# Feed-forward matmuls by one level of Strassen, in a transformer block of linear attention and a Hadamard feed-forward

## The chip, the cores and the metric

The kernel runs on one core of one Trainium2 chip, in float32. The metric is the device time of one execution in microseconds (us), the median over several runs. A profile is one more execution, with a record of every instruction; its span is close to the runs' time. Engines are named as the profile names them: PE is TensorE (matmuls), PEld its weight loads, DVE is VectorE, ACT is ScalarE, POOL is GpSimd, SP is SyncE, which here issues every DMA.

## What is computed

A sequence of 4096 tokens of width 512 goes through linear attention (16 heads of 128, 4 key/value heads), a residual and a layer norm, then a feed-forward with Hadamard transforms, a residual and a second layer norm. The attention is not touched by the change. The feed-forward of the reference, cut to what matters:

```python
def fwht(x):                      # normalised Walsh-Hadamard transform over the last dim
    ...
x = fwht(x * SU_ug) / SCALE       # 4096 x 512
x_up = x @ W_up.T * (Wscale_ug[:INTER] * SCALE)      # INTER = 2048
x_gate = x @ W_gate.T * (Wscale_ug[INTER:] * SCALE)
x = jax.nn.silu(x_gate) * x_up
x = fwht(x * SU_dp) / SCALE       # 4096 x 2048
x = x @ W_down.T * (Wscale_dp * SCALE)               # 4096 x 512
...
x = _layernorm(x + ffn(x))
```

## The kernel before

Float32 precision is had from three passes[...]: each operand is split into a high part (ScalarE copies and rounds it) and a low part (VectorE or GpSimd subtracts), and high x high, high x low and low x high are summed in PSUM. `hilo` (L89) is that split; it appears as L90 (ScalarE) and L91 (the subtraction) in the profile.

There are three stages. Attention runs first (projections at L239 for q and k with 128x256 moving operands, L192 for v, scores and state at L289 to L367); it leaves its numerators, denominators and reciprocals in DRAM (`num_d`, `den_d`, `rec_d`). Then the output projection loops over 32 tiles of 128 tokens (L610): 48 matmuls each at L622 out of resident weights, residual, first norm, and the result to `y_d` in DRAM. Beside it, GpSimd and VectorE prepare the down weights: `prep_down` (L576) transforms `W_down` along its 2048 inputs (a 128x128 Hadamard matmul at L589 and L590, then four butterfly steps on GpSimd at L598), so that the second transform is not done on activations, and puts the split weights into `wdn_d`.

The feed-forward loops over 8 blocks `f` of 512 tokens (L658), and inside over 16 tiles `it` of 128 hidden units (L661). `front` (L495) prepares a block's input: it reads `y_d`, does the 512-wide Hadamard transform by nine butterfly steps of adds and subtractions on VectorE or GpSimd (L509, L510), transposes on TensorE (L518) and splits. For each `it`, `load_wug` (L522) reads the gate/up weights and splits them, anew in every block; 24 matmuls at L682 give gate and up, ScalarE does the silu (L687), VectorE the product (L688), and the result is split and kept. At the end of a block, 192 matmuls at L707 multiply it with the resident down weights `WD`, 48 in each of four chains over the whole 2048; residual, second norm and output follow at L713 to L715. Activations of the hidden layer never leave the chip's on-chip memory.

The order on each engine is not the program's: a scheduler places the instructions by a timeline of its own, and each engine then runs its list in order, waiting on semaphores. The DMAs of all stages go through one queue, issued by SP in its own fixed order. Buffers are pools of a fixed number of tiles (`wres` has 28 tiles of 256 KB, `praw` 3), and an instruction that writes a tile waits for the last reader of the tile that was there before.

Of the kernel before, what the change touches and what calls it, by code (L numbers as in the profile page):

```python
# [21 lines left out]
TF = 512  # L22
NF = NTOK // TF
EPS_DEN = 1e-6
EPS_LN = 1e-5
# [3 lines left out]
LAG = 1  # L29


def rsqrt_small(nc, pool, v, tag):
    y = pool.tile([128, 1], F32, tag=tag + "y", name=tag + "y")
    a = pool.tile([128, 1], F32, tag=tag + "a", name=tag + "a")
    nc.vector.tensor_scalar(y.bitcast(I32), v.bitcast(I32), 1, None, ALU.logical_shift_right)
    nc.vector.tensor_scalar(y.bitcast(I32), y.bitcast(I32), -1.0, float(0x5F3759DF), ALU.mult, ALU.add)
    c, f = 3.0, 1.0
    for _ in range(3):
        nc.vector.tensor_scalar(a, y, y, v, ALU.mult, ALU.mult)
        nc.vector.scalar_tensor_tensor(y, a, c, y, ALU.subtract, ALU.mult)  # L40
        f = f * -0.5 if c == 3.0 else f / (-2.0 * c / 3.0)
        c = 3.0 / (f * f)
    nc.vector.tensor_scalar(y, y, f, None, ALU.mult)
    return y
# [3 lines left out]
def kernel(  # L48
# [28 lines left out]
    wdn_d = dram.tile([16, 128, 2, 512], F32, name="wdn_d")  # L77
# [413 lines left out]
    suug = mid.tile([128, DM], F32, name="suug")  # L491
    wsc = mid.tile([128, 2, 16], F32, name="wsc")
    Y, YT = {}, {}

    def front(pool, fpool, nb, ptr, f, t, eng):  # L495
        if t == 0:
            Y[f] = []
        y = pool.tile([128, DM], F32, tag="y", name="y")
        dma(y, y_d[4 * f + t])
        Y[f].append(y)  # L500
        yield
        a = fpool.tile([128, DM], F32, tag="fw0v" if eng is V else "fw0g", name="fw0", bufs=1)
        b = fpool.tile([128, DM], F32, tag="fw1", name="fw1", bufs=nb)
        eng.tensor_tensor(a, y, suug, ALU.mult)  # L504
        w = 1
        while w < DM:
            aa = a.rearrange("p (n r w) -> p n r w", r=2, w=w)
            bb = b.rearrange("p (n r w) -> p n r w", r=2, w=w)
            eng.tensor_tensor(bb[:, :, 0], aa[:, :, 0], aa[:, :, 1], ALU.add)  # L509
            eng.tensor_tensor(bb[:, :, 1], aa[:, :, 0], aa[:, :, 1], ALU.subtract)  # L510
            a, b = b, a
            w *= 2
        yield
        if t == 0:
            YT[f] = tuple(mid.tile([128, 4, TF], F32R, tag="yT", name=n, bufs=2) for n in ("yTh", "yTl"))
        ps = ptr.tile([128, 4, 128], F32, tag="tr", name="ps_tr")
        for k in range(4):
            T.transpose(ps[:, k], a[:, k * 128:(k + 1) * 128], idt)  # L518
        h, l = (z[:, :, t * 128:(t + 1) * 128] for z in YT[f])
        hilo(h, l, ps)  # L520

    def load_wug(it):  # L522
        w = mid.tile([128, 2, 2, 4, 128], F32R, tag="wug", name="wug_s", bufs=2)
        wf = w.rearrange("p l u k m -> p l (u k m)")
        for j in range(2):
            c = slice(j * 512, (j + 1) * 512)
            hilo(wf[:, 0, c], wf[:, 1, c], load_raw(wug[it, :, c]))
        return w

    def layer_norm(pool, x, o, tag):  # L530
        bs = pool.tile([128, 6], F32, tag="bs", name="bs")
        mv = pool.tile([128, 2], F32, tag="mv", name="mv")
        vv = pool.tile([128, 1], F32, tag="vv", name="vv")
        V.bn_stats(bs, x)
        V.bn_aggr(mv, bs)
        V.tensor_scalar(vv, mv[:, 1:2], EPS_LN, None, ALU.add)
        rs = rsqrt_small(nc, pool, vv, tag)
        V.tensor_scalar(o, x, mv[:, 0:1], rs, ALU.subtract, ALU.mult)

# [1 line left out]
    with ExitStack() as es:  # L541
        p2 = es.enter_context(tc.tile_pool(name="c2", bufs=2, reuse_waits="tile"))
        p1 = es.enter_context(tc.tile_pool(name="c1", bufs=1, reuse_waits="tile"))
# [5 lines left out]
        def norm_o(t, g):  # L549
# [3 lines left out]
            hi, lo = (p2.tile([128, 4, 128], F32R, tag="o", name=n, bufs=10) for n in ("oh", "ol"))  # L553
# [4 lines left out]
        for h in (NH - 2, NH - 1):  # L558
            WO.append(load_w(wo[h], mid, bufs=4))
        for g in range(KVH):  # L560
            norm_o(0, g)
        dma(suug, su_ug.partition_broadcast(128))
        dma(wsc, ws_ug)
        V.tensor_scalar(wsc, wsc, float(1.0 / np.sqrt(np.float32(DM))), None, ALU.mult)
        had32 = p1.tile([128, 128], F32, name="had32")
        dma(had32, had)
        hadr = p1.tile([128, 128], F32R, name="hadr")
        V.tensor_copy(hadr, had32)
        sudp = p1.tile([128, 16], F32, name="sudp")
        dma(sudp, su_dp)  # L570
        V.tensor_tensor(wsc[:, 0], wsc[:, 0], sudp, ALU.mult)
        wsdp = p1.tile([128, DM], F32, name="wsdp")
# [3 lines left out]
        def prep_down(q):  # L576
            raw = p2.tile([128, 16, 64], F32, tag="da", name="draw")
            dma(raw, wd[q])
            yield
            h = p1.tile([128, 2, 16, 64], F32R, tag="dh", name="dh")  # L580
            for j in range(2):
                c = slice(8 * j, 8 * j + 8)
                hilo(h[:, 0, c], h[:, 1, c], raw[:, c])
            yield
            a = p2.tile([128, 16, 64], F32, tag="db", name="dbf")
            for j in range(2):
                c = slice(8 * j, 8 * j + 8)
                ps = pfd.tile([128, 8, 64], F32, tag="fd", name="ps_fd")
                T.matmul(ps, hadr, h[:, 0, c], start=True, stop=False)  # L589
                T.matmul(ps, hadr, h[:, 1, c], start=False, stop=True)  # L590
                V.tensor_tensor(a[:, c], ps, wsdp[:, None, q * 64:(q + 1) * 64].to_broadcast([128, 8, 64]), ALU.mult)
            for step in range(1, 5):
                w = 1 << (step - 1)
                b = p2.tile([128, 16, 64], F32, tag="da" if step % 2 else "db", name="dbf")
                aa = a.rearrange("p (n r w) d -> p n r w d", r=2, w=w)
                bb = b.rearrange("p (n r w) d -> p n r w d", r=2, w=w)
                for r, op in ((0, ALU.add), (1, ALU.subtract)):
                    G.tensor_tensor(bb[:, :, r], aa[:, :, 0], aa[:, :, 1], op)  # L598
                a = b
            yield  # L600
            hl = p1.tile([128, 2, 16, 64], F32R, tag="dh", name="dhl")
            for j in range(2):
                c = slice(8 * j, 8 * j + 8)
                hilo(hl[:, 0, c], hl[:, 1, c], a[:, c])
            for j in range(2):
                dma(wdn_d[:, :, j, q * 64:(q + 1) * 64].rearrange("i p d -> p i d"), hl[:, j])

        fins, gd, ug = [], [], []
        starts = (0, 4, 8, 12, 16, 20, 23, 26)
        for t in range(32):  # L610
            if t + 2 < 32:
                pre(t + 2)
            else:
                ug.append(load_wug(t - 30))
# [13 lines left out]
            yt = p2.tile([128, DM], F32, tag="yt", name="yt")  # L628
            layer_norm(p2, xn, yt, "r1")
            dma(y_d[t], yt)  # L630
            if t in starts:
                gd.append(prep_down(len(gd)))
            for q, t0 in enumerate(starts):
                if t - t0 in (0, 1, 2):
# [138 lines left out]
```

## Time and profile before

| what | us |
|---|---|
| median of 3 runs | 2407.45 (2407.33 to 2408.84) |
| span of the profiled execution | 2408.2 |
| attention, to the first output projection matmul | 941 |
| output projection, to the first gate/up matmul | 376 |
| feed-forward, first of eight blocks | 150 |
| one of the later blocks | 133.65 |
| from the last matmul to the end | 7.7 |

The blocks are read from the chain of work that ended last, in which each block's first gate/up matmul can be found (1316.84, 1467.30, 1600.73, 1734.38). A "span" is from the first to the last instruction. Busy time of matmuls is modelled, since they are pipelined: a matmul of 128x512 is shown with 392 ns although the next one starts 227 ns after it. So the distance of the starts is what counts. A group of instructions is shown as line, engine, operation, output<-inputs, count, busy time, mean, and then the idle time just before it:

```
L91 DVE TENSOR_TENSOR wug_s<-raw,wug_s 128x512 fp32r<-128x512 f32 x256 | 181.3, 743 | 11.4 <-ACT wug_s L90 11.3
L688 DVE SCALAR_TENSOR_TENSOR hh<-ps_gu,wsc,sg 128x512 f32<-128x512 f32 x128 | 95.9, 749 | 269.1 <-PE ps_gu L682 267.9 <-ACT sg L687 1.2
L300 DVE TENSOR_TENSOR s<-ps_s,s 128x256 f32<-128x256 f32 x124 | 51.9, 419 | 14.7 <-PE ps_s L289 13.5
L713 DVE TENSOR_TENSOR y<-ps_dn,y 128x512 f32<-128x512 f32 x32 | 22.0, 689 | 94.4 <-PE ps_dn L707 94.1
L598 POOL TENSOR_TENSOR dbf<-dbf 128x512 f32<-128x512 f32 x64 | 97.5, 1544 | 196.7 <-DVE dbf L591 184.2 <-issue 7.2 <-DVE mv L535 4.2
L221 POOL TENSOR_TENSOR sw<-sw,csb 128x512 f32<-128x512 f32 x160 | 217.2, 1358 | 166.8 <-ACT sw L220 158.5 <-POOL A L346 1.5 <-DVE A L343 0.8
```

### The profile page before, as it was taken

To read this page: it belongs to the slowest core of one execution; us is meant where nothing else is said; L and a number is where in the kernel's file an instruction comes from. 1 tells how busy PE (TensorE), PEld (TensorE's weight loads), DVE (VectorE), ACT (ScalarE), POOL (GpSimd) and SP (SyncE) were. 2 spreads that over 40 slices of the span, in tenths; PEclk is the share of its full clock that TensorE was granted. 3 is DMA by queue.
4 is the path that set the end of the run, shared out by engine and by line. 5 is a ranking of instruction groups with operands and counts; after the bars stand their busy time and mean duration, and the time that the engine had idled before them with its cause. 6 is when DMAs were issued, how large, how long until landed. Compare 5 with 4: busy or idle time off the path is not lost.

```text
span 2408.2 us, 38221 instructions
## 1 busy us (share of the span) xinstructions
PE 2356.0 (98%) x13600; PEld 2040.2 (85%) x13600; DVE 1825.2 (76%) x3408; ACT 1106.5 (46%) x1928; POOL 848.6 (35%) x839
## 2 busy tenths in 40 slices
PE   7999999999999998999999899999999999999998
PEld 6999999999999996777888688888888888888887
DVE  6999999998888897999998847475655757475443
ACT  5777777777777774222222332314141323324140
POOL 2455454454444452684242504022220405031000
PEclk9999999999999998999999899999999999999999
DMA  6555555644554447878885532213131222223120
GB/s 181 144 157 147 176 145 151 170 132 133 140 146 137 125 135 244 285 235 274 272 275 176 177 131 76 92 60 98 44 114 59 91 70 88 83 70 95 42 92 18
DMA packets 223583, 329.97 MB, mean 137 GB/s; under 512 B 62398, under 2 KB 99328, under 8 KB 219424
## 3 DMA queue, kind: packets, MB, share of 16 engines
q1 hardware_dynamic: 223392, 327.53, 44.6%
q8 instruction: 107, 1.75, 0.3%
q14 instruction: 84, 0.69, 0.1%
HBM read 209.62 MB, written 76.02 MB: 119 GB/s over the span
## 4 chain that ended last, share of the span: by engine, by line
PE 89%; DVE 6%; DMA 2%; issue 2%; ACT 1%; POOL 0%; SPq 0%; DVEq 0%; ACTq 0%; POOLq 0%
PE ps_gu L682 28%; PE ps_qk L239 16%; PE ps_dn L707 15%; PE ps_wo L622 12%; PE ps_num L366 6%; PE ps_s L289 4%; PE ps_v L192 3%; PE ps_sc L332 1%; PE ps_den L367 1%; PE ps_sc L333 1%; DMA rb<-rec_d 1%; DVE ps_on L552 1%; PE ps_tr L518 1%; DVE fw L510 1%; PE pt L277 0%
## 5 line engine op out<-in xcount | busy, mean ns | idle before, releaser
L682 PE MATMUL ps_gu<-yTh,wug_s 128*128 128x512 f32 x2048 | 646.4, 392 | 9.8 <-DVE wug_s L91 4.1
L682 PEld LDWEIGHTS ps_gu<-yTh,wug_s 128*128 128x128 f32 x2048 | 385.8, 189 | 95.3 <-DVE wug_s L91 8.6
L682 PE MATMUL ps_gu<-yTl,wug_s 128*128 128x512 f32 x1024 | 400.6, 391 | 0.0
L239 PE MATMUL ps_qk<-xh,wh 128*128 128x256 f32 x1280 | 358.7, 280 | 5.7 <-ACT wh L90 3.9
L239 PE MATMUL ps_qk<-xl,wh 128*128 128x256 f32 x1280 | 357.0, 279 | 0.6 <-DVE xl L91 0.6
L239 PE MATMUL ps_qk<-xh,wl 128*128 128x256 f32 x1280 | 357.2, 279 | 0.0
L346 POOL TENSOR_SCALAR_AFFINE_SELECT A<-A 64x512 fp32r<-64x512 f32 x256 | 219.9, 859 | 315.5 <-DVE am L342 208.8
L707 PE MATMUL ps_dn<-wdn,hh_h 128*128 128x512 f32 x1024 | 327.9, 396 | 0.0
L688 DVE SCALAR_TENSOR_TENSOR hh<-ps_gu,wsc,sg 128x512 f32<-128x512 f32 x128 | 95.9, 749 | 269.1 <-PE ps_gu L682 267.9
L221 POOL TENSOR_TENSOR sw<-sw,csb 128x512 f32<-128x512 f32 x160 | 217.2, 1358 | 166.8 <-ACT sw L220 158.5
L90 ACT ACTIVATE wug_s<-raw 128x512 fp32r<-128x512 f32 x256 | 150.5, 626 | 230.2 <-PE ps_gu L682 192.9
L239 PEld LDWEIGHTS ps_qk<-xh,wh 128*128 128x128 f32 x1280 | 242.4, 189 | 6.9 <-ACT wh L90 4.1
L504 POOL TENSOR_TENSOR fw<-y,suug 128x512 f32<-128x512 f32 x18 | 25.1, 1393 | 633.2 <-DMA y<-y_d 603.1
L239 PEld LDWEIGHTS ps_qk<-xl,wh 128*128 128x128 f32 x1280 | 241.9, 189 | 1.8 <-DVE xl L91 0.8
L239 PEld LDWEIGHTS ps_qk<-xh,wl 128*128 128x128 f32 x1280 | 241.7, 189 | 1.1
L707 PEld LDWEIGHTS ps_dn<-wdn,hh_h 128*128 128x128 f32 x1024 | 191.6, 188 | 43.7
L682 PEld LDWEIGHTS ps_gu<-yTl,wug_s 128*128 128x128 f32 x1024 | 193.5, 189 | 40.4
L687 ACT ACTIVATE sg<-ps_gu,wsc 128x512 f32<-128x512 f32 x128 | 87.7, 686 | 264.5 <-PE ps_gu L682 264.0
L622 PE MATMUL ps_wo<-wh,ol 128*128 128x512 f32 x512 | 203.9, 398 | 1.7 <-DVE ol L91 1.7
L622 PE MATMUL ps_wo<-wh,oh 128*128 128x512 f32 x512 | 203.3, 397 | 2.2 <-ACT oh L90 2.2
L622 PE MATMUL ps_wo<-wl,oh 128*128 128x512 f32 x512 | 202.8, 396 | 0.0
L707 PE MATMUL ps_dn<-wdn,hh_l 128*128 128x512 f32 x512 | 202.1, 395 | 0.0
(122 smaller groups left out, 5116.3 us busy)
## 6 DMA issues: line engine op xcount, KB each, us to landing
raw<-in_wug_dram SPq DMA_DIRECT2D x256, 256.0 KB
vd<-vhl SPq DMA_DIRECT2D x128, 256.0 KB
num_d<-num SPq DMA_DIRECT2D x128, 256.0 KB
rb<-rec_d SPq DMA_DIRECT2D x128, 256.0 KB
nt<-num_d SPq DMA_DIRECT2D x31, 1024.0 KB
y<-y_d SPq DMA_DIRECT2D x36, 256.0 KB
raw<-in_x_t_dram SPq DMA_DIRECT2D x32, 256.0 KB
csb<-in_cs_dram SPq DMA_DIRECT2D x32, 256.0 KB
```

The costliest lines, as they stand in the source:

```text
L90: S.activation(hi, src, AF.Copy)
L192: T.matmul(ps[:, t], B[xa][:, k, t * 128:(t + 1) * 128], w[:, k % 2], start=i == 0, stop=i == 11)
L221: G.tensor_tensor(sw, sw, sinb, ALU.mult)
L239: T.matmul(ps[:, j], W[key][wa][:, k * 128:(k + 1) * 128], B[xa][:, k], start=i == 0, stop=i == 11)
L289: T.matmul(ps[:, i], B["kfn"][r, g, i // 2], B["vs"][r, i // 2, g * 128:(g + 1) * 128], start=True, stop=True)
L346: G.affine_select(ah, ah.bitcast(F32), pattern=[[0, 8], [1, 64]], compare_op=ALU.is_ge, fill=0.0, base=0, channel_multiplier=-1)
L366: T.matmul(ps[:, c2], l, r, start=i == 0, stop=i == len(ops) - 1)
L622: T.matmul(ps, l[:, h], r, start=i == 0, stop=i == 47)
L682: T.matmul(ps, w[:, wa, u, k], ya[:, k], start=i == 0, stop=i == 11)
L687: S.activation(sg, pu[0], AF.Silu, scale=wsc[:, 1, it:it + 1])
L688: V.scalar_tensor_tensor(hh, pu[1], wsc[:, 0, it:it + 1], sg, ALU.mult, ALU.mult)
L707: T.matmul(ps, l[:, ts], r, start=i == 0, stop=i == 47)
```

## The change

One level of Strassen's scheme (the variant with seven products and sums S1 to S4 of one operand, T1 to T4 of the other) replaces both feed-forward multiplications. A product of 2x2 blocks takes seven block products instead of eight.

For gate/up, the tokens are cut into 4 quarters `f` of 1024 (two halves of 512), the width into two halves of 256, and the hidden tiles into 8 pairs `p`. For a pair, each of the seven products has 2 (gate, up) x 2 (k) x 3 (high and low parts) matmuls with 512 columns. The Hadamard transform of the input is moved to the weights, which is the same product: `wprep` transforms a pair's gate/up weights (a 128x128 Hadamard matmul and one more step of width four on VectorE and GpSimd), forms the seven combinations, and `wfinish` splits them and writes them to `wop_d` in DRAM during the first quarter; later quarters read them back (`wload`). The input itself is only transposed and multiplied by its signs; `ycombine` and `yfinish` form and split its seven combinations, per quarter. Products share PSUM banks: bank a takes products 0, 2, 4 and 5 one after the other on top of each other, b 3 and 6, c 1, and their values are read in between.

The hidden activations, in the seven combinations the down product needs, are written to `hop_d` in DRAM. Down becomes a stage of its own after all quarters: 8 units of 512 tokens, seven products each, of 48 matmuls with 256 columns; its weights come from `wdop_d` (written by `prep_down`, which moves from the output projection into quarters 1 and 2), its other operand is read from `hop_d` and split again. The layer norm does two tiles at once. `combine` is one elementwise instruction, on GpSimd where no engine is named; `split` is the same as `hilo`; `u_tile` hands out one of 26 tiles of 256 KB. The attention is unchanged.

The diff, cut to its core:

```diff
+NU = 26
+NBIG = 7
...
-    wdn_d = dram.tile([16, 128, 2, 512], F32, name="wdn_d")
+    wop_d = dram.tile([8, 7, 2, 128, 512], F32, name="wop_d")
+    hop_d = dram.tile([4, 7, 2, 128, 8, 256], F32, name="hop_d")
+    wdop_d = dram.tile([7, 2, 128, 8, 256], F32, name="wdop_d")
...
-        a = fpool.tile([128, DM], F32, tag="fw0v" if eng is V else "fw0g", name="fw0", bufs=1)
-        b = fpool.tile([128, DM], F32, tag="fw1", name="fw1", bufs=nb)
-        eng.tensor_tensor(a, y, suug, ALU.mult)
-        w = 1
-        while w < DM:
...
+    def wprep(p, ptr, ptag):
+        uv = []
+        for e in range(2):
+            it = 2 * p + e
+            d = big([128, 2, 4, 128], "uv")
+            for u in range(2):
+                raw = load_raw(wug[it, :, u * 512:(u + 1) * 512])
+                h, l = u_tile(dt=F32R, name="rwh"), u_tile(dt=F32R, name="rwl")
+                split(h, l, raw, V)
+                ps = ptr.tile([128, 4, 128], F32, tag=ptag, name="ps_hw")
+                T.matmul(ps, hadr, h.rearrange("p (k m) -> p k m", k=4), start=True, stop=False)
+                T.matmul(ps, hadr, l.rearrange("p (k m) -> p k m", k=4), start=False, stop=True)
...
+                V.tensor_tensor(da[:, :, 0], pa[:, :, 0], odd, ALU.add)
+                V.tensor_tensor(da[:, :, 1], pa[:, :, 0], odd, ALU.subtract)
...
+    WKEY = ["A11", "A12", "S2", "S1", "S3", "A22", "S4"]
+    YKEY = ["B11", "B21", "T2", "T1", "T3", "T4", "B22"]
...
+    def wfinish(p):
...
+        for i, key in enumerate(WKEY):
+            h, l = (wres.tile([128, 2, 2, 128], F32R, tag="w", name=n) for n in ("woh", "wol"))
...
+                split(h, l, w[key], V)
+            ops.append((h, l))
+            for j, x in enumerate((h, l)):
+                dma(wop_d[p, i, j], x.rearrange("p u k m -> p (u k m)"))
...
+    def wload(p):
+        ops = []
+        for i in range(7):
+            hl = tuple(wres.tile([128, 2, 2, 128], F32R, tag="w", name=n) for n in ("woh", "wol"))
+            for j, x in enumerate(hl):
+                dma(x.rearrange("p u k m -> p (u k m)"), wop_d[p, i, j])
...
+    def yfinish(f, B):
...
+            for k in range(2):
+                h, l = (yop.tile([128, 512], F32R, tag="yo", name=n) for n in ("yoh", "yol"))
+                split(h, l, B[key][:, k], V if k else G)
...
+    def prep_down(qq):
...
+            h, l = (u_tile((128, 8, 64), F32R, n) for n in ("doh", "dol"))
+            split(h, l, B[key], V)
+            for j, x in enumerate((h, l)):
+                dma(wdop_d[i, j, :, :, qq * 64:(qq + 1) * 64], x)
...
+    SEQ = ("a", "c", "a", "b", "a", "a", "b")
+    for f in range(4):
+        for p in range(8):
...
+                WOPS[nxt // 8, nxt % 8] = wload(nxt % 8)
...
+            for s, tag in enumerate(SEQ):
+                first = SEQ.index(tag) == s
+                for u in (1, 0):
...
+                    for k in range(2):
+                        for wl, yl in ((0, 0), (0, 1), (1, 0)):
+                            T.matmul(ps, wops[s][wl][:, u, k], yops[s][k][yl], start=first and i == 0, stop=i == 5,
+                                     skip_group_check=not first)
+                            i += 1
+                    if s in (0, 2, 4):
+                        x = u_tile(name="sv")
+                        S.activation(x, ps, AF.Copy)
+                        sv[s, u] = x
+                    if s in (1, 6) or s == 4:
...
+                        V.tensor_tensor(x, src[0], src[1], ALU.add)
+                        emit(u, src[2], x)
...
+            def put(key):
+                i = WKEY.index(key)
+                dma(hop_d[f, i].rearrange("j p i t -> p j i t")[:, :, p], H[key].rearrange("p (j t) -> p j t", j=2))
...
+            H["S1"] = combine(u_tile(name="hS1"), a21, H["A22"], ALU.add)
+            put("S1")
...
+    def load_b(i):
...
+                x = (wres if qd % 2 else yop).tile([128, 2, 256], F32R, tag="w" if qd % 2 else "yo", name="wdo")
+                dma(x, wdop_d[i, j, :, 2 * qd:2 * qd + 2])
...
+    def a_load(n, s):
...
+        for qd in range(4):
+            raw = u_tile((128, 2, 256), name="hraw")
+            dma(raw, hop_d[f, s, jp, :, 2 * qd:2 * qd + 2])
+            h, l = (u_tile((128, 2, 256), F32R, nm) for nm in ("hah", "hal"))
+            split(h, l, raw, G if qd == 1 else V)
...
+        for ip in range(8):
+            qd, r = divmod(ip, 2)
+            for j in range(2):
+                js = slice(j * 128, (j + 1) * 128)
+                for al, bl in ((0, 0), (0, 1), (1, 0)):
+                    T.matmul(ps[:, j], ops[qd][al][:, r, js], BW[s][bl][qd][:, r], start=first and i == 0, stop=i >= 45,
+                             skip_group_check=True)
```

## The prediction

> **What bounds the kernel now.** First the page's busy times, then the chain of waits, then busy time by stage. (Durations here come from one profiled execution of 2408.2 us; the median of the runs, 2407.45, is 0.8 below it, so sums against the span carry over to the runs.)
>
> ```profile
> PE 2356.0 (98%) x13600; PEld 2040.2 (85%) x13600; DVE 1825.2 (76%) x3408; ACT 1106.5 (46%) x1928; POOL 848.6 (35%) x839
> ...
> PE ps_gu L682 28%; PE ps_qk L239 16%; PE ps_dn L707 15%; PE ps_wo L622 12%; PE ps_num L366 6%; PE ps_s L289 4%; PE ps_v L192 3%; PE ps_sc L332 1%; PE ps_den L367 1%; PE ps_sc L333 1%; DMA rb<-rec_d 1%; DVE ps_on L552 1%; PE ps_tr L518 1%; DVE fw L510 1%; PE pt L277 0%
> ```
>
> TensorE is the bound: 98% busy and 89% of the chain. The feed-forward's two lines hold 43% of it. By stage (columns: window, sum; busy us of PE, PEld, DVE, ACT, POOL; granted clock; DMA share; GB/s):
>
> ```profile
> 941.00:1317.00 376.00, 371.30 (x1586) 297.99 (x1587) 356.51 (x753) 98.27 (x169) 164.49 (x140) 0.99 0.81 260
> 1317.00:1467.00 150.00, 140.22 (x592) 112.59 (x591) 98.99 (x183) 42.02 (x69) 41.30 (x47) 0.94 0.41 135
> ...
> 1601.00:1734.00 133.00, 133.00 (x591) 108.98 (x590) 80.31 (x162) 40.42 (x68) 32.93 (x39) 1.00 0.25 80
> ```
>
> The rows are the output projection, the first feed-forward block, and a steady block. The steady one has no PE idle and a DMA share of a quarter. The chain inside it gives the spacing of the matmuls (start, us, line, count):
>
> ```profile
> 1645.77 10.88 PE ps_gu L682 x48
> 1656.65 0.23 PE ps_dn L707
> 1656.88 10.88 PE ps_gu L682 x48
> ...
> 1699.29 0.33 PE ps_tr L518 x3
> ```
>
> 49 matmuls in 11.11 us: 0.2267 each for gate/up. The down matmuls start 0.233 apart (timeline: hh_h,hh_h,hh_l at 1560.62, 1561.31, 1562.02, three each 0.70), the 128x256 projections at L239 0.1136 (499.75 to 501.00, eleven steps), a transpose 0.11. A block's period is 133.65 (1600.73 to 1734.38), which is 384 x 0.2267 + 192 x 0.233 + 16 x 0.11. The first block needs 150.5, thus 17 of entry stalls. Last, the DMA queue where it is full, and its small packets:
>
> ```profile
> DMA packets 1974, 3.59 MB, mean 359 GB/s; under 512 B 223, under 2 KB 223, under 8 KB 1973
> ...
> q1 hardware_dynamic: 1973, 3.58, 97.6%
> ...
> DMA packets 3151, 1.25 MB, mean 250 GB/s; under 512 B 2895, under 2 KB 2895, under 8 KB 3151
> ...
> q1 hardware_dynamic: 3151, 1.25, 101.6%
> ```
>
> They are the DMA views of 1325 to 1335 and 1035 to 1040. First: 1750 packets of 2 KB in 0.978 x 160 us of engine time, 89 ns each; in the quiet block 1601 to 1734 the same sum gives 103. Second: 81.3 us less 256 x 0.089, over 2895 packets of 256 B: 20 ns.
>
> **What the Trainium skill says.** "DMA: Bandwidth & Descriptors", Issuing engines are not separate DMA queues: all transfers share 16 engines; the page's single queue agrees. The same page, Why small descriptors are slow: about three cycles on top per packet, one per 32 B. That would make 1 KB cost 35/67 of 2 KB (0.79 us per 256 KB against 0.76), an estimate; the trace's only 1 KB packets (vd, vs, SBUF to SBUF; 500 to 530) cost 77 ns, 1.22 per 256 KB, so it does not agree there. "TensorE: Matmul & The Clock Gate", Part 1: a few us of idle halve the clock; the trace does this (0.50 in most of 1348 to 1355, after waits of 2.0 and 3.4 us).
>
> **The change part by part: TensorE.** Gate/up: 3072 matmuls become 4 x 8 x 7 x 2 x 6 = 2688, minus 384 x 0.2267 = 87. Down: 1536 of 512 columns become 2688 of 256: 1536 x 0.233 = 358 becomes 2688 x 0.1153 = 310 (0.1136 of L239 to 0.1167, half of down's: 305 to 314), minus 48. Hadamard on weights: 64 more 512-column matmuls, plus 14.5; the 32 of the down preparation stay, and 32 transposes per 1024 tokens stay. Of these, 32 preparation matmuls leave the output projection, 8 enter, and 16 transposes enter: it ends at 1316.8 - 5.4 + 1.8 = 1313.2. The feed-forward quarters need: f=0 672 x 0.2267 + 56 x 0.2267 + 32 x 0.11 = 168.5; f=1,2 152.3 + 16 x 0.2267 + 3.5 = 159.5; f=3 152.3. With 310 for down and 8.5 for the tail (7.7 now, from the last matmul at 2400.5; one more normalised tile), the floor without any stall is 1313.2 + 168.5 + 319 + 152.3 + 310 + 8.5 = 2271.5: 137 below the span, 17 of it the old entry stall.
>
> **DMA, which was idle and is not any more.** In units of 256 KB: 2 KB packets 0.715 (89 ns) to 0.83 (103), taken 0.76, as the stage will be full; 256 B packets 1.29 (1.2 to 1.45); the hop_d writes of 1 KB pieces 0.79 to 1.22, taken 0.9, nearer the page as they go to DRAM. Per quarter: f=0 112 wop_d writes, 28 raw, 8 y, 56 hop_d writes: 148 x 0.76 + 56 x 0.9 = 163. f=1 and 2: 112 wop_d reads, 8 wd, 8 y, 56 hop_d, 28 wdop_d writes of 256 B: 97.3 + 50.4 + 36.1 = 184 (168 to 215). f=3: 85.1 + 50.4 = 135.5. Against TensorE's 168.5, 159.5, 159.5, 152.3 the queue is the longer one in f=1 and 2, even with no bubble. In the built program each transfer waits for the one eight places before it, so the queue holds eight; I take 95% of full rate: f=1,2 193.5 each, plus 34 each over TensorE. f=0: 171.5.
>
> **The other engines, hidden or not.** VectorE at f=0, per pair of hidden tiles: 4 raw splits x 0.743, 8 half-width reads of PSUM x 0.42 (row L300), 7 splits x 0.743, 6 adds x 0.69 (L713), 4 x 0.749 (L688), 2 x 0.42: 19.5, with 0.03 between ops 20.4 of the 21.1 that TensorE takes. So nearly full while PSUM banks wait for it: 8.5 more over the quarter, f=0 180 (171 to 200). At f=1,2 it has 12 of 20. GpSimd at f=1,2: 4 combinations x 1.4 (L221 1.36, L598 1.54), preparation 64 x 1.54/16 plus 1.4, y parts 21.7/8: about 16 of 20, hidden unless hop_d waits for it. ScalarE 9 of 20. At each turn of a quarter GpSimd owes T1 to T4 (2.8 each) and 7 low parts x 1.5 beside 5.6, 27 us in the 19 of a pair: 4 exposed, three times, 12 (0 to 25). f=3: 155. Entry: wfinish, yfinish and T1 to T3 stand ahead of the products, but the slow transform of y is gone: 8 instead of 17 (3 to 20). Queued behind a waiting hop_d write on SP is every later weight load; they are placed one to two pairs early, which hides some 20 us, so only the lasting excess counts.
>
> **Down's start.** Its 56 weight tiles take the buffers that the last pair frees. From then on 56 x 0.76 + 28 x 0.76 + 10 of left hop_d writes = 74 of DMA stand against 19 + 38 of TensorE: 17 exposed (0 to 25). Afterwards a unit has 28 + 8 transfers, 27 of 38 us, and VectorE 21 x 0.743 + 7 x 0.69 + 10 = 31: hidden.
>
> Sum: 1313.2 + 8 + (180 + 193.5 + 193.5 + 155) + 12 + 310 + 17 + 8.5 = 2390.7, 17.5 under the span; I forecast 2390 us. Most of the 120 us that TensorE gains goes back in the DMA queue.
>
> **The rivals.** (1) The transfers hide: 1 KB and 2 KB packets at their low prices put f=1 at 168, and prefetch smooths it. Then quarters of 173, 163, 163, 153 and down's start at 5 give 2304 (2280 to 2345). For it: 359 GB/s seen. Against: that was only reads, for 10 us.
> (2) Slower: the queue does not hold its rate with writes, reads and eight in flight. Place: f=0 to 3. Price: at 86%, what 1100 to 1200 shows (85.5% on q1, though nothing there asked for more), quarters of 192, 214, 214, 158 give 2447; with the 1 KB price at 1.22 too, 2530. It decides from quarters summing over 740, that is f=1,2 over 203 each, 0.95 us per transfer of 212. For it: SP runs in order, and a transfer waiting for hS blocks the loads behind it. Against: loads stand early.
> (3) The seven products do not pay: reusing bank a three times makes TensorE wait for the ScalarE copy (0.59) or VectorE add; 0.35 per product, 224 times, is 78 us: 2470. Against: the built order puts two other chains between uses in most places.
>
> **How the numbers follow.** Forecast 0.42 (own range 2350 to 2430), rival 1 0.27, rival 2 0.23, rival 3 0.08. Of the forecast's case two thirds lie below 2402.6 and a fifth above 2412 (0.2% is about what a measurement tells from no change). Faster 0.42 x 0.67 + 0.27 = 0.55; same 0.05; slower 0.40. The range 2285 to 2490 leaves out the best third of rival 1 and the worst of rivals 2 and 3.
>
> **What would show it.** Right: stage rows of f=1 and 2 with DMA share above 0.9 and TensorE waiting for woh/wol loads, near 193 each, against f=3 near 155; down at 38 us a unit with a gap of 10 to 25 ahead of its first. Wrong: DMA share under 0.85 with TensorE at 100% in f=1 (rival 1), or f=1 over 205 (rival 2), or TensorE waiting for ACT or DVE within each pair (rival 3). If f=0 is far from 180, the VectorE sum failed; if down's matmuls are not 0.115 apart, the TensorE sum did.

## The result, and the profile after

The changed kernel took 2606.5 us (median of 4 runs, 2604.9 to 2620.8) against 2407.4 for the kernel before: 1.084 times as long, 95% interval 1.0815 to 1.0871. The forecast was 2390, its upper end 2490. The profiled execution has a span of 2603.8.

TensorE's busy time hardly changed, its share did. (It was to fall by 120 us; that it did not is looked at with the down stage.) These are the page's busy times and chain of waits (shares of the span by engine):

```profile
PE 2351.5 (90%) x14432; PEld 2055.3 (79%) x14432; DVE 1815.8 (70%) x3254; ACT 1213.5 (47%) x2116; POOL 981.3 (38%) x797
...
PE 74%; DMA 8%; DVE 8%; issue 5%; POOL 4%; ACT 2%; SPq 0%; DVEq 0%; ACTq 0%; POOLq 0%
```

Before, TensorE was 98% busy and carried 89% of the chain. Now no engine is full and every engine has a part in the chain, which points to time lost between engines. Where it is lost is seen by stage. The rows are the four quarters f=0 to 3 and the down stage (columns: window, sum; busy us of PE, PEld, DVE, ACT, POOL; granted clock; DMA share; GB/s):

```profile
1313.00:1567.00 254.00, 202.22 (x756) 149.80 (x755) 159.93 (x232) 103.90 (x197) 127.45 (x88) 0.91 0.61 213
1567.00:1747.00 180.00, 167.67 (x710) 133.60 (x709) 102.97 (x128) 67.59 (x116) 120.40 (x82) 0.96 0.97 306
1747.00:1933.00 186.00, 172.20 (x732) 135.42 (x731) 113.25 (x139) 68.66 (x117) 123.56 (x84) 0.96 0.95 304
1933.00:2103.00 170.00, 160.62 (x675) 128.25 (x673) 69.73 (x88) 55.37 (x91) 62.73 (x41) 0.97 0.89 293
2123.00:2595.00 472.00, 372.96 (x2688) 351.52 (x2688) 221.64 (x509) 140.43 (x224) 72.34 (x56) 0.92 0.46 151
```

Read from the first matmul of each stage in the timeline, the steps stand so against the forecast:

| step | forecast | measured |
|---|---|---|
| output projection ends | 1313.2 | 1312.2 |
| f=0 with entry | 188 | 254.6 |
| f=1, f=2, f=3 with turns | 554 | 180.9 + 185.5 + 169.2 = 535.6 |
| gap before down | 17 | 20.9 |
| down, 8 units | 310 (38.75 each) | 471.5 (50.2, then 58 to 63 each) |

Two rows hold the miss: +67 at f=0 and +161 in down. The quarters in which the DMA queue is full (shares 0.97 and 0.95) are faster than forecast; the two slow stages have it at 0.61 and 0.46. So the queue's capacity is not what failed. The gap before down is the one place where it shows: TensorE stands still, and the queue is full.

```profile
2103.00:2123.00 20.00, 0.00 (x0) 0.00 (x0) 1.25 (x2) 1.08 (x2) 5.00 (x4) 0.56 1.06 400
```

What TensorE (PE) and the DMA queue of SP wait for in the down stage (engine, line, waited for: us in total, times, longest; the longest wait of the first line, 20.5, is the gap before the stage):

```profile
PE ps_da L933 <- ACT hah L512: 35.9, 8, 20.5
PE ps_db L933 <- DVE hal L513: 29.6, 24, 1.8
PE ps_dc L933 <- ACT hah L512: 22.0, 11, 3.4
PE ps_da L933 <- DVE hal L513: 21.6, 22, 1.6
```

```profile
SPq L67 <- DVE yres L526: 166.6, 15, 14.6
SPq L67 <- PE ps_da L933: 113.7, 85, 4.1
SPq L67 <- PE ps_db L933: 38.5, 32, 1.5
```

After the gap TensorE waits 98 us in all. The stage lasts 161 us longer than forecast; most of the rest is in the matmuls themselves. The row above has TensorE busy for 373 us at a granted clock of 0.92; the same 2688 matmuls take 322 us in d3 below, where TensorE does not wait.

TensorE waits for its operand's splits, and the page's row of that split says what they wait for: `hah<-hraw`, idle 335.9, of it 299.3 for the load. The load in turn stands in SP's list behind a store of the result, which waits up to 14.6 us for the second norm. The timeline of SP between 2329 and 2368 shows one such stop (start, us, transfers):

```profile
2329.71 20.64 SPq L67 DMA_DIRECT2D hraw<-hop_d  x13
2365.07 0.81 SPq L67 DMA_DIRECT2D out_dram<-yres  x2
2365.99 0.40 SPq L67 DMA_DIRECT2D hraw<-hop_d  x1
```

Nothing is issued from 2350.35 to 2365.07, while loads stand behind the store. The remaining wait, for TensorE (`ps_da`), is one for a free tile: 26 tiles, 12 per product.

At f=0 (window 1313 to 1490) TensorE waits like this:

```profile
PE ps_hw L566 <- ACT rwh L512: 14.5, 10, 2.8
PE ps_a L812 <- ACT sv L817: 10.9, 12, 1.5
PE ps_hw L567 <- DVE rwl L513: 9.4, 10, 1.2
```

These 34.8 us in five and a half pairs, 6 a pair, are all in the preparation of the next pair or behind it: the Hadamard matmuls wait for their operands, and the products for a PSUM bank whose copy `sv` stands in ScalarE's list behind the preparation. A pair takes 31.8 us instead of the 21.1 to 22 that TensorE needs. Over the whole quarter TensorE waits 52 us and is busy for 203, at a clock of 0.91. At the spacing of f=3 (0.2333) its 728 matmuls and 32 transposes would take 173, so slower matmuls are 30 us, almost 4 a pair.

### The profile page after: what moved, and what is told of

The parts are those of the page before. It is cut to its first block, busy times and chain, and to the rows that moved or that the text cites. A ratio compares the mean times of both kernels' runs of the same rounds, so it can differ in the third digit from the quotient of the medians.

```text
span 2603.8 us, 42147 instructions
## 1 busy us (share of the span) xinstructions
PE 2351.5 (90%) x14432; PEld 2055.3 (79%) x14432; DVE 1815.8 (70%) x3254; ACT 1213.5 (47%) x2116; POOL 981.3 (38%) x797
## 4 chain that ended last, share of the span: by engine, by line
PE 74%; DMA 8%; DVE 8%; issue 5%; POOL 4%; ACT 2%; SPq 0%; DVEq 0%; ACTq 0%; POOLq 0%
PE ps_qk L246 15%; PE ps_wo L664 14%; PE ps_a L812 10%; PE ps_da L933 7%; PE ps_num L373 5%; PE ps_b L812 5%; PE ps_s L296 4%; PE ps_v L199 3%; DMA hraw<-hop_d 3%; PE ps_db L933 2%; PE ps_c L812 2%; DVE hal L513 1%; DMA wol<-wop_d 1%; PE ps_sc L339 1%; PE ps_sc L340 1%
## 5 line engine op out<-in xcount | busy, mean ns | idle before, releaser
L512 ACT ACTIVATE hah<-hraw 128x512 fp32r<-128x512 f32 x224 | 140.9, 632 | 335.9 <-DMA hraw<-hop_d 299.3
L812 PE MATMUL ps_a<-yoh,woh 128*128 128x512 f32 x512 | 214.6, 420 | 20.6 <-ACT sv L817 15.8
L933 PE MATMUL ps_da<-wdo,hah 128*128 128x256 f32 x1024 | 194.8, 291 | 36.8 <-ACT hah L512 35.9
L812 PE MATMUL ps_a<-yol,woh 128*128 128x512 f32 x512 | 209.6, 409 | 1.6 <-POOL yol L513 1.5
L812 PE MATMUL ps_a<-yoh,wol 128*128 128x512 f32 x512 | 209.0, 408 | 0.0
L97 ACT ACTIVATE oh<-ps_on 128x512 fp32r<-128x512 f32 x128 | 76.6, 599 | 274.4 <-PE ps_wo L664 179.3
L933 PEld LDWEIGHTS ps_da<-wdo,hah 128*128 128x128 f32 x1024 | 165.8, 199 | 39.1 <-ACT hah L512 39.0
L550 POOL TENSOR_TENSOR hS<-hh 128x512 f32<-128x512 f32 x64 | 91.0, 1441 | 242.6 <-DVE hh L800 212.2
L823 DVE TENSOR_TENSOR cc<-ps_b,sv 128x512 f32<-128x512 f32 x128 | 86.9, 687 | 131.5 <-ACT sv L817 129.3
L933 PE MATMUL ps_da<-wdo,hal 128*128 128x256 f32 x512 | 152.0, 297 | 24.9 <-DVE hal L513 21.6
```

Of the source, the lines that this page charges most:

```text
L512: S.activation(hi, src, AF.Copy)
L550: (eng or G).tensor_tensor(dst, a, b, op)
L812: T.matmul(ps, wops[s][wl][:, u, k], yops[s][k][yl], start=first and i == 0, stop=i == 5, skip_group_check=not first)
L823: V.tensor_tensor(x, src[0], src[1], ALU.add)
L933: T.matmul(ps[:, j], ops[qd][al][:, r, js], BW[s][bl][qd][:, r], start=first and i == 0, stop=i >= 45, skip_group_check=True)
```

## The experiments

Times are of one execution each, except for the last version; the kernel before stood at 2405 to 2410 beside them. The four executions of the changed kernel lie 16 us apart, so a smaller difference of one execution rests on the times of pairs and units in its trace. Units are the eight parts of the down stage, of seven products each, from first matmul to first matmul. Code is cut to its core, and the comments in it are added here.

**Down: what stands at the head of SP's list (pin_out).**

```diff
-            dma(out[t * 128:(t + 1) * 128], y[:, j])
+            held.append((idx + 3, t, y[:, j]))    # issued three products later
```

> Each output transfer of the down stage stands twelve loads (three products) later in SP's order, everything else as in the changed kernel. Theory A (the queue is blocked at its head: an output that waits for the second norm holds back the loads of the next products; SP waited 167 us for it): a down unit falls from 59.6 us to about 48 (seven steps of 6.9, the pace seen between the blocks), the whole to about 2520. Theory B (the 26 tiles set the pace: a load waits until TensorE frees a tile): the unit stays at 57 to 60, the whole above 2590. Theory C (bandwidth): no change either.

2569.4 (-37), units 49.0, then 54 to 56. SP's wait for the norm fell from 166.6 to 14.6, but its waits for TensorE, that is for tiles, rose from 157 to 244 in this stage:

```profile
SPq L67 <- PE ps_da L941: 132.9, 120, 2.4
SPq L67 <- PE ps_db L941: 68.7, 56, 1.5
SPq L67 <- DVE hal L513: 63.9, 59, 1.4
SPq L67 <- PE ps_dc L941: 42.7, 32, 1.5
SPq L67 <- DMA out_dram<-yres: 17.6, 13, 2.8
SPq L67 <- DVE yres L526: 14.6, 1, 14.6
```

The stop was real but covered a second one. How it cost time is not what the waits alone suggest: TensorE still waits 89 us in the stage, 9 less than before, but no wait is longer than 1.7 us, the clock is 0.99, and the same matmuls take 343 us instead of 373.

```profile
2126.20:2558.60 432.40, 343.39 (x2688) 326.89 (x2688) 223.11 (x508) 140.81 (x223) 74.66 (x56) 0.99 0.50 164
PE ps_db L941 <- DVE hal L513: 37.5, 31, 1.7
```

**Down: tiles (inplace).** The low part is written over the raw tile, 8 tiles per product instead of 12.

```diff
-            h, l = (u_tile((128, 2, 256), F32R, nm) for nm in ("hah", "hal"))
+            h = u_tile((128, 2, 256), F32R, "hah")
+            l = raw.bitcast(F32R)
```

> In the down stage the low part is written over the loaded tile, so that a product holds 8 tiles and not 12 of the 26. Theory B (tiles): a unit falls from 59.6 us to 45 or less, the whole to 2490 or less. Theory A (outputs at the head of the queue): with the same order on SP the unit stays above 54, the whole above 2560, since only the 1.3 us per step between the blocks go. Theory C (bandwidth): no change.

2535.2 (-71), units 42.7, then 48 to 53. SP still waits 149.6 for the norm here.

**Both (pin_inp).**

> The two edits of the down stage together (outputs twelve loads later on SP; low part written over the loaded tile). Alone they took 36 and 71 us off. If the head of the queue and the tiles are two waits of the same chain, a unit comes to 42 to 46 us and the whole to about 2490; if they are the same wait seen twice, it stays near the 50 us of the second alone (2535). TensorE's own 38 us are reached only if no third wait stands behind them.

2501.9 (-105, against 37 + 71 = 108 for the two alone): they add, so these are two causes. But most units stayed at 45.9, and TensorE still waited for low parts, 26.5 us between 2130 and 2450. The down stage of these versions, from its first to its last matmul (us; clock as granted):

| version | length | TensorE waits | matmuls busy | clock |
|---|---|---|---|---|
| changed kernel | 471 | 98 | 373 | 0.92 |
| pin_out | 432 | 89 | 343 | 0.99 |
| inplace | 400 | 45 | 355 | 0.95 |
| pin_inp | 366 | 31 | 335 | 0.99 |
| d3 (below) | 322 | 1 | 322 | 0.99 |

**Down: which order is left.** Outg_pl moved outputs and residual rows to GpSimd's own queue, put all low parts on VectorE, took the first raw tile of each product from an idle pool of three, and emitted loads two products ahead; the scheduler still placed them. It has inplace's edit too.

```diff
-            dma(out[t * 128:(t + 1) * 128], y[:, j])
+            G.dma_start(out[t * 128:(t + 1) * 128], y[:, j])
...
-            a_load(*order[idx + 1])
+            a_load(*order[idx + 2])
```

> The down stage of the version that writes low parts over the raw tile, with three edits: outputs and residual rows are issued by GpSimd's own queue, so that no operand load on SP stands behind them; all low parts on VectorE; the first tile of each product from the three otherwise idle raw tiles and loads emitted two products ahead. Theory A, that the loads' lead over TensorE is lost at each norm and never regained: units of 39 to 42 us, 2455 to 2480 in all. Theory B, that the limit is VectorE's order, in which low parts of the next product stand behind a sum that waits for TensorE: units stay at 45 or more, 2500 or more in all.

2515.3, units 62.7, 51.4, 50.4, 51.5, then 45 to 47: no better than pin_inp, with three edits at once. The first unit only looks slow. Its first matmul comes 1.8 us after the last one of gate/up, where the versions above have a gap of 21 to 23, and the stop stands inside it:

```profile
2120.40 0.80 PE L938 MATMUL ps_da<-wdo,hah 128*128 128x256 f32 x2 [17.18 <-ACT hah L512]
```

Why the next three units are slow was not found. d3 fixes the order of the operand loads, stores, splits and sums in this stage; its low parts are written over the raw tile too:

```diff
+    a_load(*order[idx + 3])      # loads, kept in program order on SP
+    a_split(*order[idx + 1])     # ScalarE and VectorE, kept in program order
+    if last:
+        sums(*last)              # sums of the product before, after these splits
```

> The changed kernel with the order of the down stage written out by hand: raw operands are loaded three products ahead, split (low part over the raw tile) one product ahead, and the sums of a product are taken after the splits of the next but one, so that no low part on VectorE stands behind a sum that waits for TensorE; outputs held three steps. Theory A, order on VectorE and SP is what is left: units of 39 to 42 us (45.5 with the same tiles and held outputs in the scheduler's order), 2450 to 2475 in all against 2502. Theory B, transfers' latency or the tiles bound it: units stay at 45 or above, 2495 or more.

2461.1, units 39.9, but for a first of 41.9 and a last of 40.9. The one wait of TensorE from 2130 to 2450, and the same stretch by engine:

```profile
PE ps_da L978 <- DVE yres L919: 0.9, 1, 0.9
```

```profile
2130.00:2450.00 320.00, 319.12 (x2680) 318.95 (x2678) 232.50 (x507) 127.54 (x221) 81.47 (x55) 1.00 0.67 218
```

TensorE is full at clock 1.00, with a DMA share of 0.67 and VectorE at 73%: transfers and VectorE are hidden, as forecast. loads_pin keeps only the transfers' order of d3 and gives splits and sums back to the scheduler.

```diff
-    keep = tc.keep_in_program_order
+    keep = lambda i: i
```

> d3 with only the transfers of the down stage in the fixed order (loads three products ahead, outputs held three steps); splits and sums are left to the scheduler's order. Theory A, the loads' lead on SP is what counts: units of 39 to 41 us, about 2461 to 2475. Theory B, the order on the engines (a low part behind a sum that waits for TensorE) is what counts: units of 43 to 46, 2485 to 2505.

2459.8, units 42.6, then 39.9 and a last of 40.9, the same single wait of 0.9. So, with the tiles of inplace, fixing the order of SP alone was enough: loads three products ahead, stores held back. In this version the sums' place on VectorE, the rival theory, costs nothing.

**f=0: the preparation (f0_noprep).** Pairs 1 to 7 use the weights of pair 0, which are still written to `wop_d` for each pair; the preparation of seven pairs is left out, the transfers of the products are not.

> Left out: the weights of pairs 1 to 7 are not prepared; all pairs use those of pair 0, which are written to wop_d for each pair, so that the transfers stay but for 28 raw loads. Theory A (the serial chain of the preparation, raw, split, Hadamard matmul, GpSimd's sums, split, stands in front of the products on every engine): quarter 0 falls from 254.6 us to 165 to 175, the whole to about 2525. Theory B (the queue: 112 writes of weights and 56 of hop_d): quarter 0 stays above 220.

2505.1, f=0 from 254.6 to 176.6, some 22 a pair. Of these 78 us, the 56 Hadamard matmuls that are left out are 13 of TensorE's own. TensorE's waits for the preparation are gone, and only these are left in 1313 to 1480:

```profile
PE ps_tr L544 <- DMA y_nat<-y_d: 7.4, 4, 4.2
PE ps_a L811 <- DVE yol L513: 2.5, 1, 2.5
```

**f=0: further ahead (f0_ahead).** Pairs 0 and 1 are prepared beside the output projection, and pair p + 2 in pair p.

```diff
-                gw = wprep(p + 1, pgu, "tr") if p < 7 else None
+                gw = wprep(p + 2, pgu, "tr") if p < 6 else None
```

> The weights of pairs 0 and 1 are prepared beside the output projection, and within quarter 0 a pair's combinations are formed one pair earlier than before; work and transfers are the same. Theory A (latency of the chain raw, Hadamard matmul, GpSimd's sums, split): quarter 0 falls from 254.6 us to 190 to 215. Theory B (the in-order queues: the Hadamard matmuls and their splits still stand between the products on TensorE, ScalarE and VectorE, however early their result is wanted): it stays above 235.

2606.3: nothing, although each operand is now made a pair early. Pairs with a preparation in them took 32 to 36 us, the two without 22 and 25. So it is not the length of the chain. What the traces leave is the handoffs: the lists interleave preparation and products on four engines, and a late piece stops what stands behind it. That each handoff does so is read from the waits; no run takes one of them away by itself. The timeline shows one stop and what it costs beyond itself:

```profile
1419.24 0.79 PE L816 MATMUL ps_a<-yoh,woh 128*128 128x512 f32 x1 [4.45 <-ACT sv L821]
1419.83 0.63 PE L816 MATMUL ps_a<-yol,woh 128*128 128x512 f32 x1
1420.26 0.63 PE L816 MATMUL ps_a<-yoh,wol 128*128 128x512 f32 x1
...
1422.64 0.39 PE L816 MATMUL ps_b<-yoh,wol 128*128 128x512 f32 x1
1422.87 0.40 PE L816 MATMUL ps_b<-yoh,woh 128*128 128x512 f32 x1
```

After 4.45 us of waiting the next matmuls start 0.43 to 0.59 apart, and 0.23 only some 3 us later.

**f=0: one handoff (s_on_v).** The three sums S (one is shown) run on VectorE, so that ScalarE's split of S, ahead of `sv`, does not wait for GpSimd.

```diff
-        w["S3"] = combine(mk("S3"), w["A11"], w["A21"], ALU.subtract)
+        w["S3"] = combine(mk("S3"), w["A11"], w["A21"], ALU.subtract, V)
```

> One edit to the changed kernel: the three sums S of each weight pair run on VectorE instead of GpSimd. In the trace of the changed kernel and of the one with pairs prepared earlier, TensorE waits some 6 us a pair at f=0 for a PSUM bank whose copy (sv) stands in ScalarE's queue behind the split of an S that GpSimd has not yet made. Theory A, that this one wait is the cost of f=0: it goes, 5 to 6 us on seven pairs, 2565 to 2575 us. Theory B, that any of the handoffs of the preparation stalls as much once this one is gone: 2595 or more.

2584.2 (-22), f=0 at 242, a pair at 30.8: between the two theories. f=0 explains 13 of the 22. Two pairs with other waits became 7 us shorter each, pair 5 of f=1 (28.1 to 20.8) and the last of f=2 (27.4 to 20.5), and other places became longer. In the changed kernel TensorE waits in these two pairs for rows of the next quarter (`y_nat`), 4.5 and 4.6 us. The same three waits of f=0 remain with 16.3, 9.6 and 8.3 us. The expectation put all 6 us a pair down to the wait for `sv`, which is some 2 of them, and the edit hardly shortened it (10.9 to 9.6), so this run does not say what that wait alone is worth.

**f=0: no preparation beside products at all (early7).** Pairs 1 to 7 are prepared beside the output projection, where GpSimd had nothing to do, with low parts on GpSimd, and stored; f=0 loads its weights like every other quarter.

```diff
+        def ahead():
+            for p in range(1, 8):
+                yield from wprep(p, pfd, "fd", G)
+                yield from wstore(p, G)      # splits into u tiles, to wop_d
+            yield from wprep(0, pfd, "fd")
```

> Pairs 1 to 7 are prepared wholly beside the output projection, with low parts on GpSimd, and stored; f=0 then only loads its weights, like the later quarters. Theory A, that the handoffs of the preparation stall TensorE at f=0 and nothing else does: f=0 takes 165 to 180 us (254.6 before). The output projection gets 126 transfers more, about 96 us of queue time on top of a share of 0.77 of some 320 us, so it may end up to 20 us later: 2530 to 2560 us in all. Theory B, that the work only moves its stall to the output projection, where VectorE is at 82%: the projection ends 50 us or more later, 2590 or more in all.

2538.3 (-68), f=0 at 185, of which the first pair has 36. The output projection ends at 1324.2, 12 later. TensorE waits for only 1.8 us from 1000 to 1324, so the 12 are its own 56 added matmuls (56 x 0.23 = 13):

```profile
1000.00:1324.00 324.00, 320.28 (x1386) 256.91 (x1384) 312.25 (x680) 113.95 (x213) 171.47 (x117) 1.00 0.88 311
```

VectorE is at 96% and the DMA share 0.88 there: it fits, barely.

**Turns of a quarter (y_on_v, turn).** First all low parts of the next quarter's input on VectorE, then instead its rows loaded two pairs and transposed one pair earlier, with the sums T1 to T3 ahead of the last pair.

```diff
-                split(h, l, B[key][:, k], V if k else G)
+                split(h, l, B[key][:, k], V)
```

> All low parts of the seven input combinations are subtracted on VectorE, none on GpSimd. Theory A (GpSimd's 27 us at each turn of a quarter): the first pair of quarters 1 to 3 falls from 31 to 33 us to 22 to 25, the whole by 20 to 28. Theory B (the turn waits for the transposed rows and the sums T1 to T3, which stay): it falls by under 8 in all.

2595.3; the first pairs of the quarters took 27.7, 36.8 and 28.9 us, before 30.8, 33.2 and 32.0, together 3 less. In the changed kernel TensorE does wait for a low part of GpSimd in two of them, 7.5 us at f=1 and 8.9 at f=3. With the low parts on VectorE it waits for those of VectorE (10.0 in all), so GpSimd is not what makes the turn long.

```diff
-            if f < 3 and 4 <= p:
-                for t in (2 * p - 8, 2 * p - 7):
+            if f < 3 and 2 <= p < 6:
+                for t in (2 * p - 4, 2 * p - 3):
                     front_load(f + 1, t)
...
+            if f < 3 and p == 6:
+                YB = ycombine(f + 1)
```

> The next quarter's rows are loaded two pairs and transposed one pair earlier, and the sums T1 to T3 stand ahead of the last pair. Theory A (the turn waits for rows that come at the very end and for the sums behind them on GpSimd): the first pairs of quarters 1 to 3 fall from 30.8, 33.2, 32.0 us to 22 to 25, the whole by 22 to 30. Theory B (it is the splits of the seven combinations): by under 10.

2590.3. First pairs 20.5, 20.5 and 19.6; quarters 1 to 3 took 509 instead of 536. Rows, transposes and sums moved together, so which of them made the turn long is not shown. Part was given back: pair 6 of f=0, where the rows now meet the preparation, took 41.8 instead of 31.9, f=0 4 more in all, and the down stage 4.

**Together.** all3 is pin_inp with f0_ahead and turn; combo4 has pin_inp, turn, half of early7 (pairs 1 to 4, with 5 to 7 prepared in the first four pairs of f=0), and of outg_pl the loads two products ahead and the pool of three tiles; best3 and best4 have d3, turn and early7, with the first quarter's T sums made before the output projection ends; best4 at three preparation steps a row block of the output projection instead of four.

> All edits together: down, quarter 0, turns. If the stages are independent, the savings add: with 115 from down, 45 from quarter 0 and 25 from the turns the whole comes to about 2420. Below 2407 only if down reaches 40 us a unit.

2476.0: 130 less than after, and the parts alone make 105 + 0 + 16 = 121.

> All edits that helped, together: outputs held three steps, low part over the raw tile with three more tiles and loads two products ahead, next quarter's rows two pairs earlier, and pairs 1 to 4 prepared beside the output projection with 5 to 7 at an even pace in the first four pairs. If the gains add up: f=0 at 190 to 210 us, down units of 40 to 43 us, 2380 to 2420 in all, at or just under the kernel before. If they do not, because one of the stages is bound by something not yet named: 2440 or more.

2438.8: f=0 was at 209 as expected, but the down units were 44 to 52 with a first one of 65, which again holds the gap (its first matmul comes 1.8 us after gate/up). From the last gate/up matmul to the last of down it took 404 us, all3 389. What it shares with outg_pl, loads two products ahead in the scheduler's order and the pool of three tiles, did harm here too; which of the two, no run separates.

> The down stage of d3, pairs 1 to 7 prepared beside the output projection (faster, done by its last third), the first quarter's sums taken before its end, and the next quarter's rows two pairs earlier. If the stages are separable: output projection to 1325, f=0 about 175 us, f=1 to 3 500 us as in combo4, down 8 units of 40 and 10 at the end, some 2330 to 2360. If f=0's earlier work delays the output projection by more, or the down units stay at 45: 2390 or more.

2367.8, the first version under the kernel before. Down has 42.8 and then 39.9 to 40.9 a unit. The output projection grew more than expected: gate/up starts at 1337.9, not 1325.

> best3 with the preparation of pairs 1 to 7 at three steps a row block of the output projection instead of four. Theory A, the output projection's growth beyond the 13 us of the 56 added Hadamard matmuls is VectorE running full at four steps: gate/up starts near 1325 as with the same three steps before (1324.2) and not at 1338, and the whole takes 2350 to 2360. Theory B, it is the transfers (share 0.9 in both): no change, 2365 to 2370. Against the kernel before the ratio is 0.975 to 0.985.

2361.3 (median of 5 runs, 2359.9 to 2364.3) against 2406.7 for the kernel before, ratio 0.981, interval 0.9799 to 0.9826. Gate/up starts at 1326.0 instead of best3's 1337.9, so the step rate did matter; but the first pair then took 36.3 instead of 27.6. Just ahead of that mark TensorE waited 8.6 us for the first split of the input (`yoh`) in best3 and 2.1 in best4; inside the first pair it waits for low parts of the input (`yol`), 4.7 and 8.5. 6 us were left of the 12. Its stages, in the order of those shown of after:

```profile
1326.00:1508.00 182.00, 166.98 (x703) 131.13 (x704) 99.06 (x116) 65.03 (x108) 81.36 (x52) 0.96 0.83 284
1508.00:1678.00 170.00, 166.48 (x724) 132.31 (x723) 104.19 (x134) 68.15 (x116) 122.34 (x83) 1.00 1.01 316
1678.00:1851.00 173.00, 166.24 (x722) 131.69 (x721) 106.80 (x134) 68.21 (x116) 121.81 (x83) 1.00 1.04 331
1851.00:2008.00 157.00, 156.72 (x672) 125.84 (x670) 63.97 (x85) 52.30 (x84) 47.11 (x34) 1.00 0.94 315
2029.00:2352.00 323.00, 321.74 (x2684) 321.34 (x2685) 232.96 (x507) 129.19 (x224) 82.39 (x56) 0.99 0.68 220
```

The same seven products, with the transfers of one stage and the preparation of another in a different place, fewer tiles a product in down and earlier rows at the turns, are 245 us faster than in the changed kernel.

## Why the prediction was wrong

The direction was wrong, and for a reason that none of the three rivals had. By its own steps:

- "Afterwards a unit has 28 + 8 transfers, 27 of 38 us, and VectorE 31: hidden." This step failed, with 161 us. Both amounts were about right: d3 shows a DMA share of 0.67 (27 of 38 is 0.71) and VectorE at 73% (31 of 38 is 82%), hidden, at 39.9 us a unit. What was left out is that hiding needs the load to be issued in time. SP's list put stores that wait for a norm ahead of loads (37 us), tiles for little over two products limited the lead (71), and the place of the loads in that list took the last 41 (2501.9 to 2461.1). Of the 149 us by which the stage is shorter in d3, 98 were waits and 51 matmuls slowed after them, a cost of waiting that the prediction had nowhere. The prediction did say that "SP runs in order", but only of hop_d writes in the quarters.
- "VectorE at f=0 ... with 0.03 between ops 20.4 of the 21.1 ... f=0 180". This failed with 67 us, though the sum itself held: VectorE's 159.9 us in f=0 are 20.0 a pair. The work was summed for one engine; the preparation passes among ScalarE, TensorE, VectorE and GpSimd several times, and each is also in the products' path. Without it f=0 took 176.6, where TensorE's own need is then 160 (672 x 0.2333 and the transposes). The prediction allowed 8.5 us for PSUM banks, and over the whole quarter TensorE waited 15.3 for the copies `sv` that free them. It allowed nothing for the Hadamard matmuls' waits for their operands, 30.6, nor for slower matmuls, 30.
- Turns: 4 us each were forecast for GpSimd's T sums and low parts; the first pairs took 10 to 13 more than a steady one. y_on_v shows that the low parts being on GpSimd was not it; turn, that rows, transposes and the sums T1 to T3 came too late, without telling which.
- DMA in f=1 and 2, forecast 193.5 each, was mis-sized to the high side: 180.9 and 185.5. A fit of queue time on packet counts over 1570 to 2100 gives 90 ns for 2 KB, 50 for 1 KB and 19 for 256 B. So the hop_d writes cost 0.80 per 256 KB, not 0.9. The estimate of 0.79, from the three cycles a packet that the Trainium skill gives in "DMA: Bandwidth & Descriptors", Why small descriptors are slow (HBM only), came close. The dearer 1 KB packets between buffers were the wrong row to lean on: that section exempts transfers from SBUF to SBUF from its penalty, and the 77 ns measured for them in the kernel before are a difference that it does not explain. A share of 0.95 was too careful as well; best4 has 1.01 and 1.04. Best4's quarters of 170 and 173 are nearer to rival 1's 163 than to 193.5.
- TensorE's floor was a little low: a steady pair takes 19.6 at f=3, 0.2333 a matmul and not 0.2267; a steady unit of down takes 39.9, 0.1189 a matmul, above the range of 0.1136 to 0.1167. Together, 2688 x 0.0066 and 2688 x 0.0036, some 27 us. What makes the spacing longer is open.
- What was looked for at f=1 and 2, a DMA share above 0.9 with TensorE waiting for `woh` and `wol` loads, came by half: the share was there, these waits were not. Only the rows `y_nat` of the next quarter came late, with one wait of some 4.5 us in each of the two quarters. In the steady pairs of f=2, TensorE is busy 102.73 of 104 us beside a share of 1.06:

```profile
1801.00:1905.00 104.00, 102.73 (x444) 81.21 (x443) 63.12 (x81) 40.84 (x71) 68.89 (x49) 1.00 1.06 319
```

- Right: the end of the output projection, and the gap before down (20.9 for 17, within 0 to 25), for the reason given: the queue is full in it (1.06). Rival 3 named the wait for `sv` but as a cost of every product; in f=1 to 3 steady pairs have none of it. The sum of rival 1 comes to 2308.7 rather than 2304, which changes nothing.

The sentence "Most of the 120 us that TensorE gains goes back in the DMA queue" was the wrong story: with the orders mended the queue is fuller than ever and costs TensorE little but the 22 us of the gap before down.

Left open: why outg_pl and combo4 have a slower down stage than pin_inp and all3, and why the rows come in time in s_on_v.

## What to carry to other kernels

A stage is hidden only if its first load is issued early enough: after adding up busy time, walk the in-order list of each queue and engine, and ask of every entry what it waits for and which load or copy stands behind it. Preparation that crosses several engines costs more beside a stage whose operands it delays than its busy time; put it where an engine is empty (here the output projection), whole, through DRAM if need be. A total of waits does not say what it costs: pin_out took 152 us of SP's wait for the norm away and gained 37, and of these only 9 were TensorE's waits. Beside the waits of TensorE, read how long the same matmuls take.

## What was not expected of the hardware

The DMA queue held 316 to 331 GB/s at a share of 1.01 to 1.04 for 343 us, in packets from 256 B to 2 KB, while TensorE was 96 to 98% busy at clock 1.00. Packets of 1 KB to DRAM took 50 ns, those of 1 KB between buffers in the kernel before 77. The cost of a wait on TensorE does not end with it: the down stage had a clock of 0.92 in the changed kernel, and 98 us of waits cost 149. The number and the sum of the waits do not decide this. In that stage the changed kernel had some 80 waits with 98 us, the longest 3.4 and eleven of over 2; pin_out had 76 with 89 us, none over 1.73, and kept a clock of 0.99. Nor does their length alone: f=0 of the changed kernel had 49 waits with 52 us, only two of them over 2, and a clock of 0.91. How close together waits lie was not varied by itself, so the rule stays open. The Trainium skill, "TensorE: Matmul & The Clock Gate", Part 1, has the clock halved after an idle window of about 3.4 us. This agrees in kind: after the wait of 4.45 us in f0_ahead matmuls started some 0.43 apart instead of 0.23. But the down stage of the changed kernel lost clock without a wait longer than 3.4 after its first matmul.
